# Score matmuls of 128 keys cut into two of 64 keys, on 64x64 tiles of the tensor engine

## The chip, the cores and the metric

The kernel runs on one core of one Trainium2 chip. The metric is device time in microseconds (us); lower is better. Several executions are timed for each kernel, and one more is recorded by the hardware profiler. "Faster" or "slower" needs a difference of more than 2%.

## The reference

One layer of masked graph attention with a normalisation before it, on 128 graphs of 128 nodes and 768 features, 12 heads of 64, all in float32:

```python
h = jnp.maximum(_layernorm(x, axis=-1), 0.0)
q, k, v = split_heads(h @ Wq + bq), split_heads(h @ Wk + bk), split_heads(h @ Wv + bv)
scores = einsum('bhqd,bhkd->bhqk', q, k) / sqrt(64) + beta * adj
scores = where(adj > 0, scores, -9e15)
out = x + einsum('bhqk,bhkd->bhqd', softmax(scores), v)      # (128, 128, 768)
```

## The kernel before

Four graphs are worked on at a time (`GRP`). The projections to q, k and v are matmuls of 128x128 weights with 256 moving columns, arranged as 15 products per slice instead of 18 (`product`). Between the products stand the bursts of the attention, one for each pair of heads (`oc`): `scores` and, some products later, `attend`.

```python
def scores(G, oc):                                   # 189 of these
    ...
    ps = [psum.tile([P, GRP, N], F32, tag="at", ...) for i in range(2)]      # one PSUM tile per head
    for g in range(GRP):
        t = qk[G, f"qk{u}", g // 2, j]               # head 0 on partitions 0-63, head 1 on 64-127
        at = slice((g % 2) * N, (g % 2 + 1) * N)
        for i in range(2):
            r = slice(i * HD, (i + 1) * HD)
            # weights: 128 keys; moving: 128 queries; contracted: 64 features
            nc.tensor.matmul(ps[i][:, g, :], t[r, 1, at], t[r, 0, at], start=True, stop=True)
    ...                                              # VectorE adds the bias, ScalarE takes exp: e

def attend(G, oc):                                   # 189 of these
    for r in range(2):
        for g in range(2):
            for i in range(2):
                # weights: 128 queries of e; moving: 64 columns of v and one of ones
                nc.tensor.matmul(pa[:, 2 * g + i, :], es[G, oc, i][:, 2 * r + g, :],
                                 vt[G, "v", r, h // 4][:, 4 * g + h % 4, :], start=True, stop=True)
    ...                                              # divided by the sum, added to x, stored

def attention(G, u):                                 # which burst follows which product
    for i in range(3):
        todo.setdefault(1 + 4 * i, []).append(lambda oc=3 * u + i: scores(G, oc))
        todo.setdefault(5 + 4 * i, []).insert(0, lambda oc=3 * u + i: attend(G, oc))
```

So an `attend` and the next `scores` often stand side by side (126 of 189 bursts). At the very end the last group uses half bursts (`scores_half`, `attend_half`, six of each).

## Time and profile before

| | before |
|---|---|
| time, median of 3 runs | 3119.64 us (3119.45 to 3120.21) |
| TensorE matmul busy | 99% of the span |
| VectorE / ScalarE / GpSimd busy | 64% / 26% / 12% |
| score bursts, attend bursts | 189 each, and 6 half bursts each |
| one score burst in the chain | 1.09 us, and 0.19 us more in the product behind it |

A share of 99% says that the engine has no gaps, not that its array is full. For that one has to go down to single starts. The record of a burst's first matmul begins 1 ns after that of its weight load (1526.300 and 1526.299 us) and is 373 ns long, where later ones are 272, so it includes the wait for the weights, and the spacing of the later starts is the pace. In front of a burst the records show a wait of 94 ns, called the drain below (a product matmul starts 309.7 ns before a score, 215.8 before another product). Starts in ns are from the single records of the trace; the views shown here round them to 10 ns and merge them.

### The profile page before, as it was taken

What the parts mean: (1) busy time and instruction counts of PE and PEld (TensorE: products, weight loads), DVE (VectorE), ACT (ScalarE), POOL (GpSimd) and SP (SyncE); (2) the same over time, 40 slices, a digit from 0 to 9 for tenths busy, and PEclk for the clock granted to TensorE, in tenths of its full rate; (3) what the DMA queues carried; (4) which work ended last, traced back from release to release, by engine and by line L of the source; (5) the groups of instructions that cost most, each with busy time, mean ns of one, the idle gap of its engine ahead of it and who ended that gap; (6) DMA issues with size and microseconds to landing.
All of it is one profiled execution on the core that took longest, in us unless ns stands there. A gap on an engine that the chain in (4) does not pass through costs nothing.

```text
span 3118.2 us, 46382 instructions
## 1 busy us (share of the span) xinstructions
PE 3099.8 (99%) x17846; PEld 2748.6 (88%) x17846; DVE 2000.8 (64%) x5155; ACT 801.1 (26%) x1703; POOL 375.8 (12%) x307
## 2 busy tenths in 40 slices
PE   8999999999999999999999999999999999999999
PEld 7888888888888888888888888888888888888887
DVE  7866656666566665666656666556666566665654
ACT  2222222322222222222232222222322222222221
POOL 1111111011110111111111111111011110111110
PEclk9999999999999999999999999999999999999999
DMA  5212112121122121221112212112121122111111
GB/s 154 72 48 58 41 48 65 52 54 46 44 65 58 48 55 42 57 62 49 54 40 56 65 48 58 41 48 65 52 55 44 46 65 57 49 52 40 56 35 38
DMA packets 358481, 169.94 MB, mean 54 GB/s; under 512 B 84464, under 2 KB 358128, under 8 KB 358256
## 3 DMA queue, kind: packets, MB, share of 16 engines
q1 hardware_dynamic: 355392, 166.14, 19.4%
q8 instruction: 142, 2.33, 0.3%
q10 hardware_dynamic: 2864, 0.79, 0.1%
q14 instruction: 83, 0.68, 0.1%
HBM read 116.53 MB, written 50.33 MB: 54 GB/s over the span
## 4 chain that ended last, share of the span: by engine, by line
PE 98%; DVE 1%; DMA 0%; ACT 0%; issue 0%; SPq 0%; ACTq 0%; DVEq 0%
PE pc_qk L316 18%; PE pb_qk L316 14%; PE pa_qk L316 14%; PE av L379 10%; PE pc_v L316 9%; PE pb_v L316 7%; PE pa_v L316 7%; PE pd_qk L316 7%; PE sc L355 7%; PE pd_v L316 4%; PE plain L443 1%; DMA x<-in_x_dram 0%; ACT x L259 0%; DVE A L266 0%; PE av L411 0%; PE pm L228 0%
## 5 line engine op out<-in xcount | busy, mean ns | idle before, releaser
L383 POOL TENSOR_TENSOR xo<-xo,o 128x512 f32<-128x512 f32 x189 | 258.3, 1367 | 2427.1 <-DVE seen L370 1496.1
L359 ACT ACTIVATE e<-e 128x512 f32<-128x512 f32 x378 | 231.9, 630 | 752.3 <-DVE e L358 751.6
L259 ACT ACTIVATE x<-x,shift,rstd 128x192 f32<-128x192 f32 x512 | 228.0, 533 | 588.3 <-POOL shift L250 588.3
L379 PEld LDWEIGHTS av<-v,e 128*128 128x128 f32 x3024 | 367.4, 192 | 9.8
L316 PE MATMUL pb_qk<-S,qk_T 128*128 128x256 f32 x1512 | 367.1, 386 | 0.0
L379 PE MATMUL av<-v,e 128*128 128x65 f32 x3024 | 358.2, 272 | 0.0
L337 ACT ACTIVATE qk<-pc_qk,bqk 128x256 f32<-128x256 f32 x378 | 158.1, 469 | 727.6 <-PE pc_qk L316 727.6
L358 DVE SCALAR_TENSOR_TENSOR e<-sc,biasT 128x512 f32<-128x512 f32 x378 | 243.0, 685 | 127.0 <-PE sc L355 127.0
L316 PEld LDWEIGHTS pb_qk<-S,qk_T 128*128 128x128 f32 x1512 | 277.3, 190 | 40.1
L341 DVE TENSOR_TENSOR qk<-qk,pb_qk 128x512 f32<-128x512 f32 x252 | 172.1, 683 | 162.9 <-PE pb_qk L316 144.7
L316 PE MATMUL pc_qk<-S,qk_B 128*128 128x256 f32 x1008 | 244.7, 386 | 1.2 <-ACT qk L337 1.2
L316 PE MATMUL pa_qk<-S,qk_T 128*128 128x256 f32 x1008 | 244.8, 386 | 0.0
L316 PE MATMUL pc_qk<-S,qk_T 128*128 128x256 f32 x1008 | 238.1, 379 | 0.0
L266 DVE STREAM_TRANSPOSE A<-x 128x256 f32<-128x256 f32 x384 | 217.4, 612 | 7.4 <-ACT x L259 7.3
L355 PE MATMUL sc<-qk 64*128 64x128 f32 x3024 | 219.6, 285 | 0.0
L316 PEld LDWEIGHTS pc_qk<-S,qk_T 128*128 128x128 f32 x1008 | 191.5, 190 | 26.0
L316 PEld LDWEIGHTS pc_qk<-S,qk_B 128*128 128x128 f32 x1008 | 186.3, 190 | 31.9 <-ACT qk L337 1.6
L316 PEld LDWEIGHTS pa_qk<-S,qk_T 128*128 128x128 f32 x1008 | 186.2, 190 | 30.5
L355 PEld LDWEIGHTS sc<-qk 64*128 64x128 f32 x3024 | 183.4, 187 | 29.5 <-issue 20.9
L316 PE MATMUL pb_v<-v_T,S 128*128 128x256 f32 x768 | 183.9, 382 | 0.0
L341 DVE TENSOR_TENSOR qk<-qk,pd_qk 128x512 f32<-128x512 f32 x126 | 86.6, 688 | 147.3 <-PE pd_qk L316 147.3
L367 DVE TENSOR_TENSOR o<-av,rs 128x256 f32<-128x256 f32 x384 | 160.3, 418 | 2.3 <-DVE seen L370 0.4
(117 smaller groups left out, 4516.1 us busy)
## 6 DMA issues: line engine op xcount, KB each, us to landing
x<-in_x_dram SPq DMA_DIRECT2D x504, 96.0 KB, 2.4
xo<-in_x_dram SPq DMA_DIRECT2D x189, 256.0 KB, 2.8
out_dram<-xo SPq DMA_DIRECT2D x189, 256.0 KB, 2.2
adj<-in_adj_dram SPq DMA_DIRECT2D x128, 64.0 KB, 2.3
qk_T<-in_L_gnn_Wq_dram SPq DMA_DIRECT2D x10, 128.0 KB, 3.2
qk_T<-in_L_gnn_Wk_dram SPq DMA_DIRECT2D x10, 128.0 KB, 3.1
v_T<-in_L_gnn_Wv_dram SPq DMA_DIRECT2D x5, 256.0 KB, 5.7
qk_B<-in_L_gnn_Wq_dram SPq DMA_DIRECT2D x8, 128.0 KB, 3.1
```

The costliest lines, as they stand in the source:

```text
L259: nc.scalar.activation(t, t, AF.Relu, bias=shift[G, n], scale=rstd[G, n])
L266: last = nc.vector.transpose(t[:, :, g * N:(g + 1) * N].rearrange("p c (b i) -> p c b i", i=SQ), src)
L316: nc.tensor.matmul(p[:, i, :], lhs, rhs, start=(first and i == 0 and c == 0), stop=(c == 1), skip_group_check=True)
L337: nc.scalar.activation(t[:, i, :], p[:, i, :], AF.Identity, bias=bqk[:, i, oc:oc + 1], scale=float(sign))
L341: added[G] = nc.vector.tensor_tensor(t, t, p, ALU.add if sign > 0 else ALU.subtract)
L355: nc.tensor.matmul(ps[i][:, g, :], t[r, 1, at], t[r, 0, at], start=True, stop=True)
L358: nc.vector.scalar_tensor_tensor(e, ps[i], SCORE_CAP * ISCALE, biasT[G], op0=ALU.min, op1=ALU.add)
L359: nc.scalar.activation(e, e, AF.Exp, scale=1.0 / ISCALE)
L367: nc.vector.tensor_mul(o, pa[:, :, 0:HD], rs.to_broadcast([P, 4, HD]))
L379: nc.tensor.matmul(pa[:, 2 * g + i, :], es[G, oc, i][:, 2 * r + g, :], vt[G, "v", r, h // 4][:, 4 * g + h % 4, :], start=True, stop=True)
L383: nc.gpsimd.tensor_add(t, t, o.rearrange("p a (b j) d -> p (a b) (j d)", j=2))
L443: nc.tensor.matmul(p[:, i, :], b[:, c, i * P:(i + 1) * P], a[:, c, :], start=(k == 0 and i == 0 and c == 0), stop=(c == 1), skip_group_che ...
```

## The change

The intent: a score matmul contracts only 64 rows, and two of them, on the upper and the lower half of the array, run together in the kernel before (the first two of the burst above start at 1526.300 and 1526.307 us). If the keys (the columns of the weights) are also cut into halves of 64, each matmul needs a quarter of the array, and four are to run at a time.

```diff
             for i in range(2):
                 r = slice(i * HD, (i + 1) * HD)
-                nc.tensor.matmul(ps[i][:, g, :], t[r, 1, at], t[r, 0, at], start=True, stop=True)
+                for k in range(0, N, HD):
+                    nc.tensor.matmul(ps[i][k:k + HD, g, :], t[r, 1, at][:, k:k + HD], t[r, 0, at],
+                                     start=True, stop=True)
```

## The prediction

> **What bounds the kernel now.** I read the busy shares first, then the chain that ended last, then the groups by line, and at the end the timeline of one score burst.
>
> ```profile
> PE 3099.8 (99%) x17846; PEld 2748.6 (88%) x17846; DVE 2000.8 (64%) x5155; ACT 801.1 (26%) x1703; POOL 375.8 (12%) x307
> ...
> PE 98%; DVE 1%; DMA 0%; ACT 0%; issue 0%; SPq 0%; ACTq 0%; DVEq 0%
> ```
>
> TensorE is busy for 99% of the span and 98% of the chain runs over it; the next engine, VectorE, is at 64%. The granted clock is at 9 tenths or more in all 40 slices. So a nanosecond that the scores take on TensorE is a nanosecond of the total, and what other engines do with the scores is hidden.
>
> The chain in order of time shows what one score burst (four graphs, two heads) costs there; the columns are start in us, length in us, and what ran, with its count:
>
> ```profile
> 1524.64 1.73 PE pa_qk L316 x8
> 1526.37 1.09 PE sc L355 x16
> 1527.46 1.92 PE pb_qk L316 x8
> 1529.39 1.73 PE pc_qk L316 x8
> ```
>
> The product behind the burst takes 1.92 us where an undisturbed one takes 1.73. So the burst's cost is 1.09 + 0.19 = 1.28 us. The groups say how many there are and of what form:
>
> ```profile
> L355 PE MATMUL sc<-qk 64*128 64x128 f32 x3024 | 219.6, 285 | 0.0
> L355 PEld LDWEIGHTS sc<-qk 64*128 64x128 f32 x3024 | 183.4, 187 | 29.5 <-issue 20.9
> ...
> L379 PE MATMUL av<-v,e 128*128 128x65 f32 x3024 | 358.2, 272 | 0.0
> ```
>
> 64*128 is active rows by columns of the array. The program has 189 bursts of 8 score matmuls, 1512; the trace has 3024, so each float32 matmul is carried out as two passes, each with its own weight load. All bursts together cost 189 x 1.28 = 242 us, 7.8% of the span. This is all that the change can touch.
>
> Now inside a burst. The first answer below is the stretch 1526.20 to 1527.50, the second only the 20 ns from 1526.29 to 1526.31:
>
> ```profile
> 1526.30 0.97 PEld L355 LDWEIGHTS sc<-qk 64*128 64x128 f32 x16 [0.33 <-issue]
> 1526.30 1.16 PE L355 MATMUL sc<-qk 64*128 64x128 f32 x16
> 1527.39 0.30 PEld L316 LDWEIGHTS pb_qk<-S,qk_T 128*128 128x128 f32 x2
> ...
> 1526.30 0.19 PEld L355 LDWEIGHTS sc<-qk 64*128 64x128 f32 x2 [0.33 <-issue]
> 1526.30 0.38 PE L355 MATMUL sc<-qk 64*128 64x128 f32 x2
> ```
>
> Two weight loads and two matmuls start within 20 ns: the two heads lie on rows 0 to 63 and 64 to 127 and already work side by side. The single records of the trace show the whole burst as eight such pairs; from the third start on, a pair begins 111.5 ns after the one before it (1526.514, 1526.625, 1526.737 and so on), its two members 6 to 7 ns apart. So the array is already full during the burst: two tiles of 64x128 cover all of it. This is the fact on which the prediction turns.
>
> One burst, from the end of the last product's streaming to the start of the next one's, by these records: 94 ns until the first score load (a product matmul that is followed by a score starts 309.7 ns before it, against 215.8 before another product); 107 ns for the first weight load; 8 pairs of 111.5 = 892 ns; 94 ns until the product's first load (the last score matmul starts 202 ns before the product, 107 of it streaming); 107 ns for that load. Sum 1294 ns, which agrees with the 1.28 us of the chain. Of this 8 x 106.7 = 854 ns are streaming (a product streams 256 columns in about 213 ns, so 128 columns in 106.7).
>
> [...] here the output columns are 128 and are cut into 64 by hand, so that each half needs its own pass of the same 128 moving columns. [...] the attention-times-values matmuls stream only 65 columns and still follow each other at 111.5 ns. No run yet shows 64 columns. [...] each product's load starts 1 to 2 ns after the matmul before it on the same rows and is hidden. What it means for two column tiles in the same rows is the open question below.
>
> **The change part by part.** It touches the 189 full bursts; the six half bursts at the end (another function) stay. VectorE, ScalarE and the transfers get the same instructions in the same order, and PE the same order with each score matmul doubled.
> Removed: 16 passes of 64x128 per burst. Added: 32 passes of 64x64, 8 on each of four tiles. Matmul and load records rise by 3024 each, from 17846 to 20870.
> If all four tiles run side by side, each has 8 passes, as each of two had before, and each pass still streams 128 columns: no streaming is saved. What is saved is the weight load: the first of a burst takes 53 in place of 107 ns (-54), and later passes are no longer paced by loads (106.7 + 4.8 = 111.5) but by streaming with the 2.5 ns that a product shows above its 213.3: 109.2, so 8 x -2.3 = -18 ns. Against it two more tiles that start 6 ns apart each: +12 to +18 ns. The drains stay. Sum -54 - 18 + 15 = -57 ns per burst, x 189 = -11 us: 3109 us, 0.35% less.
> A ceiling: even if everything in a burst but streaming vanished, 1294 - 854 = 440 ns x 189 = 83 us, 2.7%. Half a burst's drains and loads belong to the mode switch and the next product, which the change leaves alone, so over 2% is out of reach.
>
> **The rivals.**
> Rival 1: the two column tiles of one head don't overlap, since both take the same 64 rows of weights and moving data. Then each row half has 16 passes one after the other, 16 x 109.2 = 1747 in place of 892 ns: +855 - 54 = +800 ns, x 189 = +151 us, 3271 us, 4.8% more. [...] For it: what the trace shows is independence between row halves only.
> Rival 2: they overlap in part. The two passes of one matmul go to the same tile in succession. If instructions for the same rows start strictly in order, the second pass of the left half waits for its first, and the load of the right half behind it waits too: per matmul one load of 53 + 5 and one stream of 107 = 165 ns, 8 x 165 = 1320, and one more stream at the end: about 1427 against 892 + 54, so +0.4 to +0.5 us, x 189 = +76 to +95 us, 3195 to 3215 us. With loads pulled forward freely it is only one more step of 109 ns per burst: +37 ns, +7 us. For it: nothing in the trace excludes it. Against it: the first passes of both heads start together although a second pass stands between them in the program, so the engine does look past a blocked pass at least across rows.
> Rival 3: the issue of twice the instructions becomes the bound, 64 loads and matmuls in 1 us. Against it: a wait of the PE sequencer for the product that starts at 1575.89 is recorded at 1572.36, just behind a burst, with 32 loads and matmuls still queued; elsewhere the lead is 36. So it refilled at least 28 in the burst's 1.1 us, under 40 ns each; with 36 queued ahead, the other 28 of a burst of 64 need about 1.1 us, as long as the burst. Tight; if the queue is shorter with four tiles, add 0.1 to 0.5 us per burst, 20 to 95 us.
> VectorE does not take over: it reads a pair of full score banks as before, and idles for a third of the time.
>
> **Range and chances.** I give full overlap, or all but a step of it, 60%: 3098 to 3128. Partial or no overlap, or an issue bound, 39%: 3140 to 3280, most of it above 3180. Nothing points below 3058, so 1% for faster. The point stays near the first case, moved a few us up for the others: 3114 us. The range, 3096 to 3275, spans both cases.
>
> **What would show it.** Right: 6048 score loads and matmuls; four starts within some 25 ns, repeated every 109 to 125 ns; a burst of about 1.03 us in the chain with the product behind it still at 1.92; score loads of well under 187 ns. Rival 1 shows as starts in twos at 109 ns over 1.8 us; rival 2 as steps of about 165 ns[...]. The prediction is wrong if the drain around a burst grows with the finer mode, or if a burst gets shorter than its 854 ns of streaming.

## The result, and the profile after

| | before | after |
|---|---|---|
| median | 3119.86 us (4 runs) | 3107.78 us (4 runs, 3107.53 to 3110.16) |
| ratio after / before | | 0.9963, 95% interval 0.9946 to 0.998: within 2% |

The busy shares of the kernel after, to be read beside the first line that the prediction shows:

```profile
PE 3087.6 (99%) x20870; PEld 2730.2 (88%) x20870; DVE 1999.2 (64%) x5155; ACT 800.2 (26%) x1703; POOL 375.9 (12%) x307
```

TensorE has 3024 more matmuls and 3024 more weight loads, and is busy for 12 us less. The other engines have the same counts. The chain in order of time (start us, length us, what ran) shows the same neighbours as before:

```profile
1519.89 1.03 PE sc L356 x32
1520.92 1.93 PE pb_qk L316 x8
1522.85 1.73 PE pc_qk L316 x8
```

Twice the matmuls take 1.03 us where half as many took 1.09, and the product behind a burst still pays 0.19 to 0.20 us. So the whole gain, about 0.06 us, is inside the burst. The groups by line (busy us, mean ns of one, then idle time before and what ended it) give the new form, and the view of the score tile gives durations in ns (shortest, median, longest):

```profile
L356 PE MATMUL sc<-qk 64*64 64x128 f32 x6048 | 208.7, 276 | 0.0
L356 PEld LDWEIGHTS sc<-qk 64*64 64x64 f32 x6048 | 162.9, 133 | 29.4 <-issue 20.9
...
L356 PEld LDWEIGHTS sc<-qk x6048: 129/133/134, 77.7 to 3071.2; 64*64 64x64 f32 x196
L356 PE MATMUL sc<-qk x6048: 268/269/322, 77.7 to 3071.4; 64*64 64x128 f32 x196
```

The loads are shorter, 133 ns where they were 187 to 188: 54 ns less. In the single records the second load on a tile starts 108 ns after the first one before (1526.299 and 1526.407 us), and 55 ns after it here (1519.819 and 1519.874), so half the columns load in half the time. The recorded length of a matmul (269 against 272) is no measure of its streaming: those of e1 stream half as many columns and show 272 too. The spacing of the starts is. And the timeline of the 50 ns at the start of a burst shows that all four tiles begin together:

```profile
1519.82 0.15 PEld L356 LDWEIGHTS sc<-qk 64*64 64x64 f32 x4 [0.33 <-issue]
1519.82 0.34 PE L356 MATMUL sc<-qk 64*64 64x128 f32 x4
```

In the single records of this burst the four first matmuls start at 1519.821, .827, .834 and .841, the next four from 1519.981, and then a group of four every 109.2 ns (1520.090, .199, .308, .417, .527, .636). Laid beside the burst of before:

| part of a burst, ns | before | after | difference |
|---|---|---|---|
| first start to the second start on the same tile (first load and first streaming) | 214 | 160 | -54 |
| six more steps | 6 x 111.6 | 6 x 109.2 | -14 |
| last tile starts behind the first one by | 6.7 | 20 | +13 |
| last score matmul to the product's first | 202 | 199 | -3 |
| **sum** | | | **-58** |

The product or attend matmul in front of a burst keeps its distance (309 and 205 ns, before and after). In both traces the 189 bursts agree with each other within 1 ns, so 58 ns x 189 = 11.0 us. The medians differ by 12.1 us. In the two profiled runs (spans 3118.2 and 3105.7 us) the first burst also starts 1.4 us earlier after (77.7 against 79.1 us); 11.0 and 1.4 make up 12.4 of the 12.5 us between the spans. The first products of the run after follow each other every 216 ns from 16.4 us on, those of the run before every 427 ns until 18.8 us, which makes up the 1.4 us. In the second series of runs of the changed kernel (e8 below) they are at 427 ns too, until 19.1 us, and the first burst starts at 78.9 us, so that this part is not the change's. It goes with the clock: from 14.6 to 19.0 us the granted clock is 0.62 in e8 and 1.00 after (the trace of before has records of it only from 19.0 us on).

### The profile page after: what moved, and what is told of

It is laid out like the page before. It is cut to its first block, busy times and chain, and to the rows that moved or that the text cites. A ratio compares the mean times of both kernels' runs of the same rounds, so it can differ in the third digit from the quotient of the medians.

```text
span 3105.7 us, 52430 instructions
## 1 busy us (share of the span) xinstructions
PE 3087.6 (99%) x20870; PEld 2730.2 (88%) x20870; DVE 1999.2 (64%) x5155; ACT 800.2 (26%) x1703; POOL 375.9 (12%) x307
## 4 chain that ended last, share of the span: by engine, by line
PE 98%; DVE 1%; DMA 0%; ACT 0%; issue 0%; SPq 0%; ACTq 0%; DVEq 0%
PE pc_qk L316 18%; PE pb_qk L316 14%; PE pa_qk L316 14%; PE av L381 10%; PE pc_v L316 9%; PE pb_v L316 7%; PE pa_v L316 7%; PE pd_qk L316 7%; PE sc L356 6%; PE pd_v L316 4%; PE plain L445 1%; DMA x<-in_x_dram 0%; ACT x L259 0%; DVE A L266 0%; PE av L413 0%; PE pm L228 0%
## 5 line engine op out<-in xcount | busy, mean ns | idle before, releaser
L356 PE MATMUL sc<-qk 64*64 64x128 f32 x6048 | 208.7, 276 | 0.0
L356 PEld LDWEIGHTS sc<-qk 64*64 64x64 f32 x6048 | 162.9, 133 | 29.4 <-issue 20.9
```

Of the source, the lines that this page charges most:

```text
L356: nc.tensor.matmul(ps[i][k:k + HD, g, :], t[r, 1, at][:, k:k + HD], t[r, 0, at], start=True, stop=True)
```

## The experiments

Each kernel differs from before or after by the edit shown. All of them gave correct results.

### e8: the changed kernel again

No edit, five rounds, because the gain is small.

> The changed kernel again, with more rounds, to size a gain of some 0.4 per cent. The trace says 58 ns per burst x 189 = 11.0 us, so 3108.5 us if nothing else moved. If the gain were a chance of the first runs it would lie within 3 us of before.

Measured: 3108.85 us (3108.0 to 3110.66), before 3119.01, ratio 0.9967 (0.9953 to 0.9981). The gain is real and is 10 to 12 us; the trace's 11.0 lies between the two series.

### e1: the other cut, 64 queries instead of 64 keys

```diff
-                nc.tensor.matmul(ps[i][:, g, :], t[r, 1, at], t[r, 0, at], start=True, stop=True)
+                for k in range(0, N, HD):
+                    nc.tensor.matmul(ps[i][:, g, k:k + HD], t[r, 1, at], t[r, 0, at][:, k:k + HD],
+                                     start=True, stop=True)
```

> The kernel before with each score matmul cut the other way: 64 of the 128 moving columns (queries) each, all 128 keys as weights, two row tiles as before. My theory says that a pass costs the longer of its weight load and its streaming: 16 passes on each row tile, each paced by its 128-column load, 111.5 ns, so 1784 in place of 892 ns per burst, +0.89 us x 189 = +169 us: about 3288 us. The rival, that a pass costs what it streams and small matmuls are as good as large ones, says 16 x 56 = 896 ns and 3120 us.

Measured: 3286.41 us, ratio 1.0535 (1.0518 to 1.0553). The chain of this run:

```profile
1524.77 1.98 PE sc L356 x32
1526.75 1.92 PE pa_qk L316 x8
```

A burst takes 1.98 us where it took 1.09, though it streams the same number of columns. From its first to its last matmul there are 1778 ns against 890. So in these runs a pass costs the longer of its load and its streaming, and halving the streaming alone brings nothing: the pace stays that of the 128-column loads (about 112 ns in the records, 111.6 before with 128 columns streamed), and there are twice as many. That the time came within 2 us of the forecast is partly luck: the first streaming of a burst is 53 ns shorter (half of the 106.6 ns for 128 columns, worked out below), which I had not counted, and the second head loses 41 ns at its fifth pass, whose load starts only at 501 ns, 5 ns after the first head's fifth matmul. This is the rule that e3 and e9 bring out below.

### e2: 32 keys per matmul, eight tiles

```diff
-                for k in range(0, N, HD):
-                    nc.tensor.matmul(ps[i][k:k + HD, g, :], t[r, 1, at][:, k:k + HD], t[r, 0, at],
+                for k in range(0, N, 32):
+                    nc.tensor.matmul(ps[i][k:k + 32, g, :], t[r, 1, at][:, k:k + 32], t[r, 0, at],
```

> The changed kernel with 32 keys per matmul: eight tiles of 64x32, 64 score matmuls per burst in place of 32, 128 load and matmul records. My theory: streaming still sets the pace, 8 passes per tile at 109 ns; the first load falls from 53 to 27 ns and eight tiles start 6.7 ns apart instead of four (+27 ns), so nothing is left to gain: 3108 us, within 4 us of the changed kernel. The rival, issue as the bound: with some 36 records queued ahead, the other 92 at up to 40 ns each need up to 3.7 us, at 16 ns each 1.5 us, so 0.4 to 2.6 us more per burst: 3185 to 3600 us.

Measured: 3121.72 us, ratio 1.0007 (0.9991 to 1.0024). Both expectations missed: it is 14 us slower than the changed kernel, and far from the rival's hundreds. (The 16 ns of the rival is the rate that the changed kernel shows: 64 loads and matmuls in a burst of 1.03 us.) The chain:

```profile
1527.38 1.09 PE sc L356 x64
1528.47 1.92 PE pb_qk L316 x8
```

From first to last matmul a burst takes 888 ns against 835, +53 ns, which is 10 us over 189 bursts. Up to 482 ns into the burst the matmuls start in groups of eight, 6.7 ns apart, every 109 ns, as expected; there are 36 of them by then. After that many starts are 16 to 17 ns apart (588, 604, 621, 638, 654 in the burst at 1527.31). The loads show it first: 33 have started by 355 ns, and the next comes at 436. From there each further tile gets its fifth load 16 to 17 ns after the tile before it, while loads as a whole come every 9 ns (15 between 436 and 564 ns), since one turn of a tile is two loads and two matmuls. Why is open. It may be the rate at which loads and matmuls are handed to the engine, or a limit on how many it holds: in all 189 bursts the pause comes after 33 loads and 32 matmuls. No run tests either. The changed kernel has half as many in a burst, and its groups of four come on time. The remaining 4 us are not in the bursts; 1.6 of them lie in front of the first burst, as in the run before.

### e3: the same matmuls, tile after tile

```diff
-        for g in range(GRP):
-            ...
-            for i in range(2):
-                for k in range(0, N, HD):
+        for i in range(2):
+            for k in range(0, N, HD):
+                for g in range(GRP):
+                    ...
```

> The changed kernel with the score matmuls of a burst in another order: all four graphs on one tile, then on the next tile, so that 16 loads and matmuls of one tile stand in a row. It asks how far the engine looks past blocked instructions. If each tile has its own deep queue, nothing changes: 3108 us. If the engine sees about 36 records ahead, the first two tiles run together and the fourth can start only after some three steps, so 0.33 to 0.44 us more per burst: 3170 to 3190 us. If matmuls start strictly in program order, the tiles run one after the other, 32 passes of 109 ns: +2.6 us per burst, about 3600 us.

Measured: 3383.73 us, ratio 1.0848 (1.083 to 1.0866). None of the three numbers came true. The chain:

```profile
1503.53 2.49 PE sc L356 x32
1506.03 1.92 PE pa_qk L316 x8
```

In the burst at 1503.46 the first loads of the four tiles start at 0, 493, 987 and 1480 ns. The fifth matmul of the first tile starts at 489, that of the second at 982, of the third at 1476. So each tile starts just when the one issued before it begins the fifth of its eight passes, whichever rows or columns it is on. The burst is 2295 ns from first to last, 1460 more than after, and 1460 x 189 = 276 us, which is the whole difference.

### e7: the kernel before, head after head

```diff
-        for g in range(GRP):
-            ...
-            for i in range(2):
+        for i in range(2):
+            for g in range(GRP):
+                ...
```

> The kernel before with all four graphs of one head issued before the other head, so 16 loads and matmuls of one row half stand in a row. The run with the tile order changed showed each further tile starting only when the one before it began its fifth of eight passes, 493 ns late, across rows as across columns. If that look-ahead per tile is the rule, the second row half starts 493 to 500 ns late here too: +0.5 us x 189 = +93 us, 3213 us. If row halves are free of each other and only column halves block, nothing changes: 3120 us.

Measured: 3221.59 us, ratio 1.0329 (1.0314 to 1.0345).

```profile
1509.74 1.64 PE sc L355 x16
```

The mechanism held and the size was off. The second head's load starts at 555 ns, the first head's fifth matmul at 550. I had carried over 493 ns from tiles with 64-column loads; here the fifth pass comes after 107 + 4 x 111 ns. 1438 - 890 = 548 ns x 189 = 104 us, measured 102.6. It also shows that matmuls of different tiles do not start in program order: the records of head 1's first two matmuls start at 556 (with the 107 ns of its load its weights are there by some 662, an estimate) and 769, those of head 0's last two, which stand in front of them in the program, at 774 and 885 ns.

### e9: two graphs in a row on each tile

```diff
+        for p in range(0, GRP, 2):
+            for i in range(2):
+                for k in range(0, N, HD):
+                    for g in (p, p + 1):
+                        ...
```

> The changed kernel with two graphs in a row on each tile (four passes) before the next tile. In the run with four graphs in a row and in the one with one head after the other, the next tile started just when the fifth of eight passes began, as if a tile took one running pass and three waiting ones, and a further one blocked everything behind it. By that rule four passes in a row never block: 3108 us, within 3 us of the changed kernel. If instead any run of passes on one tile blocks in proportion (a fixed look-ahead of about six loads and matmuls over all tiles), each further tile starts about one pass late at both rounds, +0.2 to +0.4 us per burst: 3145 to 3185 us.

Measured: 3120.26 us, ratio 1.0004 (0.9988 to 1.0021). Missed again, by 12 us, and between the two expectations. In the burst at 1526.10 the four tiles start together (first matmuls at 2, 15, 28 and 42 ns), which a look-ahead of six loads and matmuls over all tiles would not allow. But at the second round the first tile starts its fifth pass on time, its load at 382 and its matmul at 489, while the other three get their loads for it only at 493, 507 and 520. That is the rule of e3 again: the first tile's eighth pass finds room only when its fifth begins, and everything behind it waits until then, including the other tiles' fifth loads. I had applied the rule to the first round alone. So these three lose some 44 ns each, and the tiles stand 13 ns apart instead of 6.7 (+20 ns for the last); first to last is 898 ns against 835, 63 ns x 189 = 12 us. The three orders together say that in these runs a tile takes four passes, the running one and three more, and a fifth holds up all that follows (until 489 ns here and in e3, 550 in e7). That two passes in a row, as in the change, never block follows from the same rule, and the change's trace agrees. The rule is inferred from tiles of 64x64 and 64x128; for the eight tiles of e2 it is not shown.

### e4: half of each burst cut

```diff
-                for k in range(0, N, HD):
-                    nc.tensor.matmul(ps[i][k:k + HD, g, :], t[r, 1, at][:, k:k + HD], t[r, 0, at],
+                step = HD if g < 2 else N
+                for k in range(0, N, step):
+                    nc.tensor.matmul(ps[i][k:k + step, g, :], t[r, 1, at][:, k:k + step], t[r, 0, at],
```

> The changed kernel with only the first two graphs of a burst cut into 64 keys and the other two in 64x128 tiles, so that one more change of tiling mode lies inside each burst. My theory: that change costs a drain of 94 ns and an exposed first load of 107 ns, and four passes are back at 111.5 (+9): +210 ns per burst against the changed kernel, +40 us: about 3148 us. The rival, that only a change of the rows drains and a change of columns doesn't, says half of the change's gain, 3114 us.

Measured: 3148.61 us, ratio 1.0095 (1.0078 to 1.0111), as expected and 35 us from the rival. In the chain:

```profile
1539.85 1.24 PE sc L357 x24
1541.09 1.92 PE pb_qk L316 x8
```

One more change of tiling mode, from 64x64 to 64x128, costs 1.24 - 1.03 = 0.21 us. In the records, the last matmul of the cut half starts at 400 ns, the first load of the other half at 598: 107 ns of streaming and 91 of drain (the wait between the end of streaming and the next load), then the exposed load. A change of the column cut drains like a change of the row cut, which costs 94 ns in front of a burst (309.7 - 215.8).

### e5: the cut where the load is the longer half

The theory says that column tiles shorten loads and nothing else. Then they should pay in `attend`, which loads 128 columns and streams only 65: its starts are 111.5 ns apart before, but the first two of a burst only 57 (1534.403 and 1534.460 us), about what streaming 65 columns takes. This is the kernel before with:

```diff
-                    nc.tensor.matmul(pa[:, 2 * g + i, :], es[G, oc, i][:, 2 * r + g, :],
-                                     vt[G, "v", r, h // 4][:, 4 * g + h % 4, :], start=True, stop=True)
+                    for k in range(0, N, HD):
+                        nc.tensor.matmul(pa[k:k + HD, 2 * g + i, :], es[G, oc, i][:, 2 * r + g, k:k + HD],
+                                         vt[G, "v", r, h // 4][:, 4 * g + h % 4, :], start=True, stop=True)
```

> The kernel before with the scores as they were, and the attention-times-values matmuls cut in two instead, 64 queries as weights each, on two column tiles of 128x64. There a pass streams only 65 columns (54 ns) but loads 128, so before it is paced by its load at 111.5 ns. My theory (column tiles pay where the weight load is the longer half of a pass): 16 passes per tile at 53 + 5 = 58 ns, 930 in place of 1784 ns per burst, -855 ns x 189 = -162 us; against it the new changes of tiling mode: 63 bursts between products pay 94 + 53 in front and 94 + 107 behind (+348 ns, 22 us), 126 that a score burst follows pay 94 + 53 in front (+147 ns, 19 us). Sum -121 us: about 2999 us. The rival, that two column tiles share the load path so that loads of the same rows queue up, leaves 111.5 ns per pair of halves and adds the drains: 3150 to 3160 us.

Measured: 3007.92 us (3007.57 to 3008.94), ratio 0.9644 (0.963 to 0.9659): faster. The chain and the groups of this run:

```profile
1524.62 1.08 PE av L380 x32
1525.70 1.09 PE sc L355 x16
1526.80 1.92 PE pa_qk L316 x8
...
L380 PE MATMUL av<-v,e 128*64 128x65 f32 x6048 | 217.9, 224 | 0.0
L380 PEld LDWEIGHTS av<-v,e 128*64 128x64 f32 x6048 | 191.8, 137 | 62.9 <-issue 43.0 <-ACT qk L337 19.9
```

An attend burst takes 1.08 us in the chain where the chain of before has 1.73:

```profile
1534.57 1.73 PE av L379 x16
1536.30 1.09 PE sc L355 x16
```

From its first to its last matmul it is 934 ns against 1620. The gain is 10 us smaller than expected, and most of that lies in the 126 bursts that a score follows. By the records, from the last product matmul to the score behind it, 215.8 + 1620 + 205 = 2041 ns became 309.7 + 934 + 149 = 1393: -648 ns, where I had -855 + 147 = -708. I took 16 x 111.5 = 1784 ns for the old burst, but there its first load is hidden behind the product in front (it starts 2 ns after that product's last matmul, 1534.189 and 1534.187 us) and its last pass streams only 54 ns (an estimate: 65 of the 128 columns that take 106.6 ns, as worked out below). For the 63 lone ones, up to the product's second matmul, 2218 ns became 1712: -506, as forecast (-855 + 348 = -507). Sum -82 - 32 = -114 us; measured -111. About 2.6 us, an estimate, were lost again in one place near the start: a gap is 1.1 us longer there, and seven steps behind it take 427 ns instead of 216 (last section).

### e6: both cuts

The changed kernel with the edit of e5.

> The changed kernel (64 keys per score matmul) and the cut of the attention-times-values matmuls together. My theory: the two gains lie on the same chain and add, 2999 - 12 = 2987 us. The rival, that a switch from 128x64 straight to 64x64 tiles costs more than one from 128x128, or that issue falls behind where 32 + 32 matmuls stand in a row, would make the second gain vanish: 2999 us or more.

Measured: 2998.52 us, ratio 0.9614 (0.9599 to 0.9628). This is 11.5 us above the forecast, because that started from the 2999 us expected of e5. The second gain is 9.4 us on top of e5, close to the 10 to 12 us that it brought alone. The times of e5 and e6 are of the same rounds, so the two cuts add. That the time lies beside the rival's 2999 is chance. Its dearer switch did not occur: behind the last attend matmul, whose streaming takes 54 ns (the estimate of e5), the score starts after 149 ns with 64x64 tiles (e6) as with 64x128 (e5).

### e10: both cuts, one change of mode less

```diff
-            todo.setdefault(5 + 4 * i, []).insert(0, lambda oc=3 * u + i: attend(G, oc))
+            if u == 1 or i < 2 or G + 1 == NG:
+                todo.setdefault(5 + 4 * i, []).insert(0, lambda oc=3 * u + i: attend(G, oc))
+        if u == 1:
+            todo[1].insert(0, lambda: attend(G, 2))
```

> The kernel with both cuts, and the last attention-times-values burst of the first half of the heads moved next to the first score burst of the second half, so that 31 of the 63 lone pairs of bursts share one change of tiling mode. In the trace of the kernel with both cuts a lone burst pays 94 ns in front (309.7 - 215.8) and 104 ns in the product behind (320 - 216), 198 ns x 31 = 6 us: 2992 us. The rival, that the moved burst delays VectorE or the release of its banks so that the next scores wait, gives 2998 us or more.

Measured: 2991.72 us (2990.68 to 2992.68), ratio 0.9592 (0.9576 to 0.9608). It is 4.1% faster than before and the fastest kernel, 6.8 us below e6 where 6 were expected (the two are of different rounds, whose before differ by 0.6 us). Of the 189 score bursts 157 now follow an attend directly, where 126 did. Its chain shows both kinds of place, an attend burst with a score burst right behind it and one that is still alone:

```profile
1508.01 1.08 PE av L382 x32
1509.09 1.03 PE sc L356 x32
1510.13 1.93 PE pc_qk L316 x8
...
1526.45 1.08 PE av L382 x32
1527.54 1.92 PE pb_qk L316 x8
```

## Why the prediction was right

**The bound.** TensorE stayed the bound at 99%, and what changed on it came out in the total: 58 ns x 189 in the trace, 10 to 12 us in the time.

**The array was already full.** This was the step that decided the size, and the trace after shows it: 32 matmuls on four tiles need as many steps of about 109 ns as 16 on two. A burst is still seven steps and one first streaming long. e1 is the check from the other side: the pace hangs on the longer of load and streaming, about 112 ns a pass with 64 columns streamed as with 128.

**The terms.** First load: forecast -54, measured -54 ns. No run had shown the 53 ns for 64 columns then; the records after show 55, and 108 for 128. Pace: 109.2 ns, forecast and measured. It acts on six steps and a last one, -14 and -3, where I wrote eight, -18. Skew of the tiles: forecast +12 to +18, measured +13. Sum -57 forecast, -58 measured. The 213 ns of streaming per 256 columns had no source in the prediction; the runs bear it out, since 215.8 ns for 256 columns and 109.2 for 128 leave 106.6 for 128 columns and 2.6 fixed. The 11 us worked out there gave 3109 us. The point was 3114, because I moved it towards rivals that did not occur. The range, 3096 to 3275, held the rivals too, so that hitting it shows little; what speaks for the mechanism are the terms.

**The drains.** They stayed: 309 and 205 ns to the neighbour in front, before and after. e4 puts a price on one more change of mode, 0.21 us.

**Rival 1, no overlap of column tiles**, did not occur, though only row halves had been seen to overlap before: four starts within 20 ns. **Rival 2, overlap in part**, did not occur for the order of the change, but it was a real danger. With four passes in a row on a tile it costs 12 us (e9), with eight 276 us (e3). The rule is not the one I argued with (a second pass blocks its rows). By the traces of e3, e7 and e9 it is room for four passes per tile, and a fifth blocks all. **Rival 3, issue**, did not bind: the groups of four start on time every 109.2 ns. With twice as many matmuls in a burst something does bind (e2), and whether that is issue stays open.

**Where the intended gain is.** A column tile of 64 halves the load (55 ns for 108). For scores the loads were hidden behind streaming nearly everywhere (the pace fell from 111.6 to 109.2 ns alone), except at the first of each burst. For attend they were the pace (111.5 ns for 65 columns streamed), and there the same cut was worth ten times as much (e5).

## What to carry to other kernels

Before cutting matmuls for more tiles, look at the spacing of single starts and ask which half of a pass sets it. Cutting the weights' columns paid where the load is longer than the streaming (111 us in e5), and hardly where two row tiles already stream side by side (11 us here). Issue the tiles in turn with one float32 matmul (two passes) at a time on each, since two in a row already cost the whole gain here (12 us, e9), and gather matmuls of one tiling mode, since a change of mode cost 0.21 us with the load behind it (e4).

## What else the records show of TensorE

- Matmuls on different tiles did not start in program order: in e7 head 1's second matmul starts at 769 ns, and two that stand in front of it in the program start at 774 and 885 ns. The step between tiles at the start of a burst was 6.7 ns with two passes in a row on each tile and 13 ns with four (e9), so 3.3 ns per pass. Weight loads also run under matmuls on the same rows: those of the products start 1 to 2 ns after the matmul before them throughout.
- A 64x64 or 64x128 tile took the running pass and three more, and a fifth held up all tiles behind it: the loads of the next tile started at 493, 987 and 1480 ns (e3) and at 555 ns (e7), each 4 to 5 ns after a fifth pass began.
- The drain at a change of tiling mode is 91 to 94 ns here, and 0.21 us in all with the load that becomes visible (e4).
- On eight tiles starts were 6.7 ns apart within a group and 13.7 ns on average (109.2 / 8, e2).
- In e5 there is a gap of 2.7 us in the first group, where a product waits for ScalarE to empty a bank. For the 3 us behind it the granted clock was 0.52 and products followed each other every 427 ns instead of 216. e6 and e10 show the same behind gaps of 2.8 us in that place. Before, the gap in the same place was 1.6 us and the clock stayed at 1.00. The windows of e5 (busy us of each engine, then the clock):

```profile
93.00:96.00 3.00, 0.79 (x4) 0.36 (x2) 3.00 (x8) 1.84 (x4) 1.27 (x1) 1.00 0.07 21
96.00:99.00 3.00, 2.91 (x7) 2.38 (x8) 3.00 (x6) 0.04 (x1) 0.00 (x0) 0.52 0.66 186
```
